# A four-layer graph kernel on one core: unread products in TensorE's first waits, layer 0's layernorms tied to mix copies, the first LSTM differences in a free tile, x loaded one group per iteration

## The chip, the cores and the metric

The kernel runs on one core of one Trainium2 chip. The core has five engines with instruction queues of their own: TensorE (PE in the profile, with its weight loads as PEld), VectorE (DVE), ScalarE (ACT), GpSimd (POOL) and SyncE (SP), which here only issues DMAs. The metric is the device time of one execution in microseconds, as a median over runs. All numbers are float32, and each float32 product is two instructions in the profile.

## The reference, cut to what matters

x is 128 graphs of 64 nodes with 256 features; adj is one 64 x 64 matrix for all graphs. Four layers follow each other, each as `x = x + layer(relu(layernorm(x)))`:

```
layer 0:  h = relu(adj @ (h @ Wg0 + bg0));  h = relu(adj @ (h @ Wg1 + bg1))
          for p in 1..4: an LSTM over windows of p nodes; its last state replaces each window's last node
layer 1:  4-head attention, masked by adj == 0
layer 2:  A_hat = normalized (adj + 1);  h = relu(batchnorm((A_hat @ h) @ W1.T + b1))
          out = batchnorm(h @ W2.T + b2)
layer 3:  w = adj * adj;  relu(w @ (h W1)), relu(w @ (h W2)), w @ (h W3)
```

## The kernel before, in words

The 8192 tokens lie as 16 groups (`NG`) of 512: a group is a tile of 128 partitions (two graphs of 64 nodes) x 4 token tiles (`GT`) x 256 features. Every stage loops over the 16 groups.

Products with a 64 x 64 matrix are made by `mix` (line 144, its two PSUM banks evicted at line 157): 32 small products, two batches side by side. Most large products use seven block products in place of eight (`seven`, lines 164 to 194): products 1, 5, 6 and 7 go to four PSUM banks, 1 and 5 are copied out at lines 173 and 174, and products 2, 3 and 4 follow in `finish`. Their operands need sums or differences of blocks, made on VectorE by `differences` (lines 198 to 202) or `sums` (206 to 209).

A layernorm is `ln_scale` followed by `ln_apply`: on VectorE four statistics (line 92), four aggregates (94), an addition (95); on GpSimd a power (96); on VectorE the shift (98); then four activations on ScalarE (111). A layernorm that is given `between` has its shift issued behind the instruction that `between` returns.

**Order.** The order on each engine is not that of the text. A list scheduler in the build gives each engine the first ready instruction by its own clock, and `tc.issue_after(ins)` puts what a block issues on ins's engine behind ins, as order alone and not as a wait. [...]SP's DMAs are in such a list as well.

**Layer 0's graph part** is a software pipeline (lines 465 to 471). In iteration g TensorE's text is: mix of group g (`first_mix`), second weights of group g-2 (line 453), second mix of group g-1 (line 144 again), first weights of group g (line 429). `first_mix` also holds the layernorm of its group. The first weights are followed by an addition on VectorE (437) and a relu on GpSimd (438), the second ones by an addition on VectorE (458) and a relu on ScalarE (461). All layernorms from group 2 on are put behind the first mix's copy alone. Before the loop, `by_batch` (297) turns adj, which comes in two DMAs, and `row_sums` (311 to 316) makes sums of it.

**The LSTMs** (line 507 on TensorE) read their differences from a tile of pool `dp`, which lies where the graph part's pools lay.

**The attention** has one iteration per group. ScalarE copies half the values out of PSUM (795, one buffer `vt`), and SP issues four 64 KB DMAs (798) that rearrange them into `v`; twice per iteration. Groups 4 to 15 of x are loaded again (512 KB each, line 58): four loads stand ahead of the loop and one in each of iterations 0 to 7. An iteration adds the LSTM result to x of group g+3 (`to_residual`) and makes the layernorm of group g+2; scores (814), exponentials (834), their transposes (850) and the weighted values (863) follow.

**Layer 2** starts in the attention's end: normalize (`activated`), mix, hidden products (735).

**Layer 3** starts while batchnorm's results (`outs`) are still being normalized (1083 on ScalarE, 1085 on VectorE), turned back (1095) and added to x (1103). `bring(n, ahead)` turns back and adds n groups and normalizes `ahead` more. `second_weights` (1222) is two sets of seven products; its differences t1 to t4 are made on VectorE. `finish` adds the last result (1301, 1308) and stores x (1304, 1309).

Of the kernel before, what the change touches and what calls it, by code (L numbers as in the profile page):

```python
# [8 lines left out]
F32 = mybir.dt.float32  # L9
# [5 lines left out]
P = 128  # L15
D = 256
NODES = 64
NTOK = 8192
GT = 4
# [5 lines left out]
NK = PER  # L25
# [13 lines left out]
def adj_preln_kernel(ctx: ExitStack, tc: tile.TileContext, x_in, adj, vec, bg0, bg1,  # L39
# [231 lines left out]
    with tc.tile_pool(name="lw", bufs=5) as lw:  # L271
# [6 lines left out]
        with tc.tile_pool(name="gw", bufs=1) as gw, tc.tile_pool(name="gcn", bufs=2) as gp, \  # L278
# [8 lines left out]
                )  # L287
            load_x(xs[1], 1)
            nc.sync.dma_start(out=vecs, in_=vec)
            ones = sp.tile([NODES, P], F32, tag="ones", name="ones")  # L290
            nc.vector.memset(ones, 1.0)

            def by_batch(ps, rows):

                for b in range(2):
                    blk = slice(b * 64, b * 64 + 64)
                    nc.tensor.matmul(
                        ps[blk, :], lhsT=rows[blk, :], rhs=ident[blk, blk], start=True, stop=True
                    )

            pt = bank((P, NODES))
            by_batch(pt, arow)
            lns = [
                ln_scale(xs[0][:, 0:2], lambda: nc.vector.tensor_copy(adj2, pt), 2),
                ln_scale(xs[0][:, 2:4], None, 2),
# [3 lines left out]
            def row_sums():  # L309
                pt1 = bank((P, NODES))  # L310
                nc.tensor.matmul(
                    pt1, lhsT=ones, rhs=adj2[0:NODES, :], start=True, stop=True
                )
# [54 lines left out]
                load_x(xs[g], g)  # L368
            w_next = (load_w(wih, 0), None)

            first_copied, first_scalar, middle_copied, turned = None, None, None, None

            def first_mix(g):
                nonlocal first_copied, middle_copied, first_scalar, turned
                h = gp.tile([P, GT, D], F32, tag="h", name="h")
                if g == 0:
                    for k, (rstd, nmr, _) in enumerate(lns):
                        two = slice(2 * k, 2 * k + 2)
                        ln_apply(xs[0][:, two], h[:, two], rstd, nmr, 2, (1,) if k else ())
                elif g == 1:  # L380
                    with tc.issue_after(first_copied):
                        rstd, nmr, _ = ln_scale(xs[1])
                    with tc.issue_after(first_scalar):
                        ln_apply(xs[1], h, rstd, nmr)
                    with tc.issue_after(first_copied):
                        row_sums()
                else:
                    if g < NK:
                        x = xs[g]
                    else:  # L390
                        x = gp.tile([P, GT, D], F32, tag="x", name="x", bufs=3)
                        load_x(x, g)
                    with tc.issue_after(first_copied):
                        ln_relu(x, h)
                m0 = gp.tile([P, 2, GN], F32, tag="m0", name="m0")
                if g == 0:


                    def on_scalar_first(*args):
                        nonlocal first_scalar  # L400
                        last = nc.scalar.copy(*args)
                        first_scalar = last.ins
                        return last

                    copied = mix(h, adj2, 2, m0, (on_scalar_first, on_vector))
                    first_copied = copied
                    with tc.issue_after(copied):
                        nc.vector.tensor_scalar(rb0[:, 0, :], rb0[:, 0, :], rsum, None, ALU.mult)
                else:
                    copied = mix(h, adj2, 2, m0, (on_vector, on_vector))  # L410
                if g == NG // 4:

                    with tc.issue_after(copied):
                        adjacency_forms()
                        turned = normalized_adjacency()
                if g == NG // 2:
                    middle_copied = copied
                    turned()
                return m0
# [23 lines left out]
                mix(h1, adj2, 2, m1, (on_scalar, on_vector if last else on_scalar))  # L443
                return m1

            def second_weights(g, m1):

                dst = hs[g // PER][:, :, :, (g % PER) * GB : (g % PER + 1) * GB]
                for m in range(2):
# [303 lines left out]
    with tc.tile_pool(name="att", bufs=2, reuse_waits="tile") as ap_:  # L753
# [136 lines left out]
        for g in range(NG):  # L890
# [105 lines left out]
    behind = [[], [], counted]  # L996
    for g in range(1, NG):
        if g == 1:
            mixed(2, (on_scalar, on_vector))
            behind.append(counted_next + hidden(1, w1, range(2, 4)))  # L1000
            continue
        if g + 1 < NG:
            with tc.issue_after(behind[g - 1][-1].ins if behind[g - 1] else after_attention):
                pool = ar_right if g + 1 < NG // 2 else keep if g + 1 == NG // 2 else ar_left
                activated(pool, g + 1, (lambda: behind[g][1]) if behind[g] else None)
                mixed(g + 1, (on_scalar, on_vector))
        if g == 3:
            for a in range(2):
# [286 lines left out]
    def finish(g, pss):  # L1295
        if g == NG - 1:

            for k in range(2):
                for q in range(2):
                    xt = xs[g][:, 2 * k + q, :]  # L1300
# [14 lines left out]
    def bring(n, ahead):  # L1315
# [14 lines left out]
    for g in range(NG + 1):  # L1330
# [78 lines left out]
```

## Time and profile before

| | |
|---|---|
| median of 3 runs (lowest, highest) | 2487.9 us (2487.6, 2489.17) |
| the profiled execution: device time | 2489.57 us |
| the profiled execution: span, first to last instruction | 2487.6 us |
| TensorE busy | 2450.4 us, 99% of the span |
| VectorE, ScalarE, GpSimd busy | 1512.0, 1149.8, 439.3 us |
| DMA | 48.00 MB, mean 19 GB/s |

A line of the timeline gives the start in us from the span's start, the busy time in us, engine, line, operation, tiles, shape and the number of instructions that were merged into it; in brackets stands the idle time of that engine before it and what ended the idle time. A line of the waits gives the waiting engine with its tile and line, what it waited for, then the sum in us, the number of times and the longest one.

### The profile page before, as it was taken

The page shows a single profiled execution, that of the slowest core. Times are in us where ns is not written, and L with a number is a line of the kernel's source. Part 1 is how long each engine was busy: PE and PEld are TensorE (multiplying, and loading weights), DVE is VectorE, ACT ScalarE, POOL GpSimd, SP SyncE. Part 2 cuts the span into 40 slices and gives each one's busy share as a digit, 9 for nine tenths or more (in the row PEclk, how much of TensorE's full clock was granted, in tenths as well). Part 3 has the DMA queues.
Part 4 walks back from the last instruction along what each step waited for, and adds up shares of the span by engine and source line. Part 5 has one row for each costly group of instructions (what it writes and reads, how often), then busy time and mean ns, then how long its engine had stood idle before and what let it go on. Part 6 is the DMA issues. An engine that isn't in the chain of part 4 may idle for free.

```text
span 2487.6 us, 46271 instructions
## 1 busy us (share of the span) xinstructions
PE 2450.4 (99%) x19626; PEld 2070.3 (83%) x19626; DVE 1512.0 (61%) x2703; ACT 1149.8 (46%) x2034; POOL 439.3 (18%) x368
## 2 busy tenths in 40 slices
PE   7999999999999999999999999999999999999999
PEld 5668888889999998888888864446998898888888
DVE  6658876666566565566589986425555455454544
ACT  4547754444455343344556566754333323333332
POOL 4422211111111111121134331003011111101110
PEclk9999999999999999999999999999999999999999
DMA  3200000001000000000311110010000000000000
GB/s 115 103 2 1 1 18 1 1 1 35 1 1 1 1 1 1 1 13 1 103 47 38 38 36 2 1 59 1 10 10 18 10 10 10 18 10 10 18 9 18
DMA packets 48527, 48.00 MB, mean 19 GB/s; under 512 B 3649, under 2 KB 44737, under 8 KB 48321
## 3 DMA queue, kind: packets, MB, share of 16 engines
q1 hardware_dynamic: 47616, 44.49, 5.8%
q8 instruction: 154, 2.52, 0.4%
q10 hardware_dynamic: 704, 0.56, 0.1%
q14 instruction: 53, 0.43, 0.1%
HBM read 28.26 MB, written 8.39 MB: 15 GB/s over the span
## 4 chain that ended last, share of the span: by engine, by line
PE 87%; DVE 7%; ACT 2%; POOL 2%; issue 1%; DMA 0%; SPq 0%; DVEq 0%; POOLq 0%; ACTq 0%
PE ps L507 40%; PE ps L1222 16%; PE ps L1267 8%; PE ps L1055 4%; PE ps L735 4%; PE ps L144 3%; PE ps L1186 3%; PE ps L429 2%; PE ps L453 2%; PE ps L768 2%; PE ps L790 1%; ACT arena L219 1%; DVE st L92 1%; POOL rstd L96 1%; POOL arena L180 1%
## 5 line engine op out<-in xcount | busy, mean ns | idle before, releaser
L507 PE MATMUL ps<-diff,s 128*128 128x256 f32 (+1 forms) x1824 | 393.5, 371 | 0.9 <-DVE diff L623 0.9
L1222 PE MATMUL ps<-arena 128*128 128x256 f32 x1792 | 392.6, 381 | 1.6 <-DVE arena L200 1.6
L1222 PEld LDWEIGHTS ps<-arena 128*128 128x128 f32 x1792 | 338.0, 190 | 55.7 <-issue 11.2
L507 PEld LDWEIGHTS ps<-diff,s 128*128 128x128 f32 x1824 | 346.0, 190 | 33.7 <-issue 1.6
L521 ACT ACTIVATE gates<-gates,lbias 128x512 f32<-128x512 f32 (+5 forms) x426 | 244.2, 621 | 202.5 <-DVE gates L185 146.9
L180 POOL TENSOR_TENSOR gates<-p 128x512 f32<-128x512 f32 (+1 forms) x115 | 149.2, 1297 | 882.1 <-DVE p L177 831.1
L507 PE MATMUL ps<-h,w 128*128 128x256 f32 (+1 forms) x1028 | 241.3, 371 | 1.6 <-ACT p L173 1.6
L507 PE MATMUL ps<-diff,w 128*128 128x256 f32 (+1 forms) x1040 | 238.7, 371 | 0.0
L507 PEld LDWEIGHTS ps<-diff,w 128*128 128x128 f32 x1040 | 197.4, 190 | 18.1
L507 PEld LDWEIGHTS ps<-h,w 128*128 128x128 f32 x1028 | 194.7, 190 | 20.8 <-ACT p L173 2.0
L521 ACT ACTIVATE gates<-ps,lbias 128x256 f32<-128x256 f32 (+3 forms) x213 | 91.7, 476 | 247.3 <-PE ps L507 247.2
L219 ACT ACTIVATE arena<-arena 128x512 f32<-128x512 f32 (+1 forms) x160 | 88.6, 582 | 195.2 <-POOL arena L180 103.2
L180 POOL TENSOR_TENSOR arena<-arena 128x512 f32<-128x512 f32 x64 | 73.1, 1143 | 530.6 <-DVE arena L177 530.6
L1267 PE MATMUL ps<-arena 128*128 128x128 f32 x1280 | 149.7, 276 | 0.0
L185 DVE TENSOR_TENSOR gates<-p,ps 128x512 f32<-128x512 f32 (+1 forms) x115 | 76.3, 664 | 120.2 <-PE ps L507 120.2
L1267 PEld LDWEIGHTS ps<-arena 128*128 128x128 f32 x1280 | 145.5, 192 | 1.1
L96 POOL TENSOR_TENSOR rstd<-rstd,mhalf 128x4 f32<-128x4 f32 (+1 forms) x66 | 66.4, 1006 | 412.1 <-DVE rstd L95 402.9
L185 DVE TENSOR_TENSOR arena<-arena,ps 128x512 f32<-128x512 f32 x64 | 39.7, 621 | 152.1 <-PE ps L1222 87.4
L176 DVE TENSOR_TENSOR p<-p,ps 128x512 f32<-128x512 f32 (+1 forms) x131 | 86.6, 661 | 51.2 <-PE ps L507 51.2
L507 PE MATMUL ps<-state,w 128*128 128x256 f32 (+1 forms) x512 | 116.1, 370 | 0.9 <-ACT p L173 0.8
L735 PE MATMUL ps<-arena,w 128*128 128x512 f32 x256 | 114.3, 599 | 1.9 <-ACT arena L157 1.9
L507 PE MATMUL ps<-state,s 128*128 128x256 f32 (+1 forms) x512 | 115.8, 369 | 0.0
(203 smaller groups left out, 4022.7 us busy)
## 6 DMA issues: line engine op xcount, KB each, us to landing
x<-in_x SPq DMA_DIRECT2D x27, 512.0 KB, 5.4
v<-vt SPq DMA_DIRECT2D x128, 64.0 KB, 2.1
out<-x SPq DMA_DIRECT2D x15, 512.0 KB, 2.9
w<-in_wih SPq DMA_DIRECT2D x4, 1024.0 KB, 7.4
w<-in_whh SPq DMA_DIRECT2D x3, 1024.0 KB, 6.0
arena<-in_l3w SPq DMA_DIRECT2D x3, 1024.0 KB, 5.1
w<-in_wqkv SPq DMA_DIRECT2D x1, 768.0 KB, 4.6
x<-in_x SPq DMA_DIRECT2D x2, 256.0 KB, 3.0
```

What stands on the lines that cost most here:

```text
L96: nc.gpsimd.tensor_tensor(out=rstd, in0=rstd, in1=mhalf[:, 0:n], op=ALU.pow)
L144: last = nc.tensor.matmul(pss[b][half * 64 : half * 64 + 64, c, t, :], lhsT=src[rows, t, col : col + 64], rhs=a2[rows, :], start=True, sto ...
L176: nc.vector.tensor_tensor(p1, p1, ps[2], ALU.add)
L180: nc.gpsimd.tensor_tensor(out=out[1][1], in0=p1, in1=p5, op=ALU.add)
L185: nc.vector.tensor_tensor(out[0][1], p1, ps[1], ALU.add)
L219: nc.scalar.activation(o, o, func)
L507: nc.tensor.matmul(ps[:, r], lhsT=wc[:, j, :], rhs=bc, start=first and r == 0 and c == 0, stop=True, skip_group_check=True,)
L521: nc.scalar.activation(o, ps, func, bias=lbias[:, col : col + 1])
L735: nc.tensor.matmul(ps, lhsT=w1[:, c, m * P : (m + 1) * P], rhs=a[:, 2 + c, :], start=(c == 0), stop=(c == 1),)
L1055: nc.tensor.matmul(pss[m], lhsT=w2[c // 2][:, c % 2, m * P : (m + 1) * P], rhs=a[:, c, :], start=(c == 0), stop=(c == 3),)
L1222: nc.tensor.matmul(ps[:, r, :], lhsT=w[:, c, col : col + P], rhs=b[:, c, :], start=first and r == 0 and c == 0, stop=c == 1, skip_group_ch ...
L1267: nc.tensor.matmul(ps[:, t, :], lhsT=w[:, c, t * P : (t + 1) * P], rhs=b[:, c, :], start=first and t == 0 and c == 0, stop=c == 3, skip_gr ...
```

## The change

It has eight edits, in the order of the program.

1. `ones` gets 128 partitions, and `keep_busy` issues products of `ones` with itself into a bank that nobody reads: seven ahead of `by_batch`, three behind its first product, two behind its second.
2. The layernorm of group g (from 2 on) is put on VectorE behind the second copy of mix g-2 (group 2's: behind group 1's shift), and its shift behind the second copy of mix g-1.
3. In iteration 16 the second weights of group 14 are cut in two, with the second mix of group 15 between the halves.
4. The differences of the first two LSTM units (p = 1) go into the tile "arena" of pool `keep`, which is free then.
5. Of x one group is loaded ahead of the attention, and group g+5 in iteration g.
6. Layer 2's mix of group 2 has both copies on ScalarE, and the later groups' work on ScalarE is put behind them.
7. In layer 3 `bring(2, 1)` after the first second mix becomes: turn the ready groups back into four banks there, and add them to x behind the differences of `second_weights`. Groups 5, 6 and 7 are normalized half on VectorE; before, both halves were ScalarE's.
8. The last group is stored in four DMAs of 128 KB, by turns from SP and from ScalarE, and no longer in two of 256 KB from SP.

```diff
-            ones = sp.tile([NODES, P], F32, tag="ones", name="ones")
+            ones = sp.tile([P, P], F32, tag="ones", name="ones")
...
-            def by_batch(ps, rows):
+            def by_batch(ps, rows, between=lambda b, last: None):
...
+                    between(b, last.ins)
+            idle = bank((P, P))
+            def keep_busy(n, behind=None):
+                with tc.issue_after(behind) if behind else nullcontext():
+                    for _ in range(n):
+                        nc.tensor.matmul(idle, lhsT=ones, rhs=ones, start=True, stop=True)
+            keep_busy(7)
             pt = bank((P, NODES))
-            by_batch(pt, arow)
+            by_batch(pt, arow, lambda b, last: keep_busy(3 - b, last))
...
-                        rstd, nmr, _ = ln_scale(xs[1])
+                        rstd, nmr, second_ln = ln_scale(xs[1])
...
-                    with tc.issue_after(first_copied):
-                        ln_relu(x, h)
+                    with tc.issue_after(second_ln if g == 2 else copied_of[g - 2].ins):
+                        ln_relu(x, h, lambda: copied_of[g - 1])
...
+                def on_vector_last(*args):
+                    copied_of.append(nc.vector.tensor_copy(*args))
+                    return copied_of[-1]
...
-                    copied = mix(h, adj2, 2, m0, (on_vector, on_vector))
+                    copied = mix(h, adj2, 2, m0, (on_vector, on_vector_last))
...
-            def second_weights(g, m1):
+            def second_weights(g, m1, ms=range(2)):
...
-                if m1 is not None:
-                    second_weights(g - 2, m1)
+                before = m1
+                if before is not None:
+                    second_weights(g - 2, before, range(1 if g == NG else 2))
                 m1 = second_mix(h1, g == NG) if h1 is not None else None
+                if g == NG:
+                    second_weights(g - 2, before, [1])
...
-                tt = dp.tile([P, 4, 2, 256], F32, tag="diff", name="diff")
+                pool, tag = (keep, "arena") if p == 1 and places[0] == units[0] else (dp, "diff")
+                tt = pool.tile([P, 4, 2, 256], F32, tag=tag, name="diff")
...
-        if g < 2 * NK:
+        if g == NK:
             load_x(xs[g], g)
...
-            if g + 2 * NK < NG:
-                load_x(xs[g + 2 * NK], g + 2 * NK)
+            if g + NK + 1 < NG:
+                load_x(xs[g + NK + 1], g + NK + 1)
...
-            mixed(2, (on_scalar, on_vector))
+            mixed_in = mixed(2, (on_scalar, on_scalar))
...
-                activated(pool, g + 1, (lambda: behind[g][1]) if behind[g] else None)
+                with tc.issue_after(mixed_in):
+                    activated(pool, g + 1, (lambda: behind[g][1]) if behind[g] else None)
...
-                two = slice(2 * k, 2 * k + 2)
-                t0 = g * GT + 2 * k
-                nc.sync.dma_start(out=out_view[:, t0 : t0 + 2, :], in_=xs[g][:, two, :])
+                    queue.dma_start(out=out_view[:, g * GT + t, :], in_=xt)
...
-                normalize(ready, on_scalar=range(2 if ready < NG // 2 else 1))
+                normalize(ready, on_scalar=range(2 if ready < 5 else 1))
...
             if g == 0:
-                bring(2, 1)
+                later = [(b, [bank((P, 2, D)) for _ in range(2)]) for b in range(brought, ready)]
+                for b, pss in later:
+                    turn_back(b, pss)
+                brought = ready
...
             h2, behind = second_weights(m1, h1)
+            if g == 0:
+                with tc.issue_after(behind):
+                    for b, pss in later:
+                        add_back(b, pss)
+                bring(0, 1)
             bring(1, 1)
```

More of the change, by code (lines that the diff above doesn't have):

```diff
@@ L289, in adj_preln_kernel @@
             nc.sync.dma_start(out=vecs, in_=vec)
-            ones = sp.tile([NODES, P], F32, tag="ones", name="ones")
+            ones = sp.tile([P, P], F32, tag="ones", name="ones")
             nc.vector.memset(ones, 1.0)
-            def by_batch(ps, rows):
+            def by_batch(ps, rows, between=lambda b, last: None):
                 for b in range(2):
                     blk = slice(b * 64, b * 64 + 64)
-                    nc.tensor.matmul(
+                    last = nc.tensor.matmul(
                         ps[blk, :], lhsT=rows[blk, :], rhs=ident[blk, blk], start=True, stop=True
                     )
+                    between(b, last.ins)
[5 more added lines that the diff above has]
+            keep_busy(7)
             pt = bank((P, NODES))
-            by_batch(pt, arow)
+            by_batch(pt, arow, lambda b, last: keep_busy(3 - b, last))
             lns = [
@@ L311, in row_sums @@
                 nc.tensor.matmul(
-                    pt1, lhsT=ones, rhs=adj2[0:NODES, :], start=True, stop=True
+                    pt1, lhsT=ones[0:NODES, :], rhs=adj2[0:NODES, :], start=True, stop=True
                 )
@@ L369, in adj_preln_kernel @@
             w_next = (load_w(wih, 0), None)
-            first_copied, first_scalar, middle_copied, turned = None, None, None, None
+            first_copied, first_scalar, middle_copied, turned, second_ln = [None] * 5
+            copied_of = []
             def first_mix(g):
-                nonlocal first_copied, middle_copied, first_scalar, turned
+                nonlocal first_copied, middle_copied, first_scalar, turned, second_ln
                 h = gp.tile([P, GT, D], F32, tag="h", name="h")
@@ L403, in on_scalar_first @@
                         return last
-                    copied = mix(h, adj2, 2, m0, (on_scalar_first, on_vector))
+                    copied = mix(h, adj2, 2, m0, (on_scalar_first, on_vector_last))
                     first_copied = copied
@@ L444, in second_mix @@
                 return m1
-            def second_weights(g, m1):
+            def second_weights(g, m1, ms=range(2)):
                 dst = hs[g // PER][:, :, :, (g % PER) * GB : (g % PER + 1) * GB]
-                for m in range(2):
+                for m in ms:
                     ps = bank((P, GB, NODES))
@@ L1298, in finish @@
             for k in range(2):
-                for q in range(2):
-                    xt = xs[g][:, 2 * k + q, :]
+                for q, queue in enumerate((nc.sync, nc.scalar)):
+                    t = 2 * k + q
+                    xt = xs[g][:, t, :]
                     nc.vector.tensor_tensor(xt, xt, pss[q][:, k, :], ALU.add)
-                two = slice(2 * k, 2 * k + 2)
-                t0 = g * GT + 2 * k
-                nc.sync.dma_start(out=out_view[:, t0 : t0 + 2, :], in_=xs[g][:, two, :])
+                    queue.dma_start(out=out_view[:, g * GT + t, :], in_=xt)
             return
```

## The prediction

> **What bounds the kernel now.** I read the page first, then TensorE's waits, then the timeline around each of them.
>
> ```profile
> span 2487.6 us, 46271 instructions
> PE 2450.4 (99%) x19626; PEld 2070.3 (83%) x19626; DVE 1512.0 (61%) x2703; ACT 1149.8 (46%) x2034; POOL 439.3 (18%) x368
> ...
> PE ps L297 <- DMA arow<-in_adj: 4.7, 2, 3.9
> PE ps L429 <- DVE m L157: 3.9, 2, 2.3
> ...
> PE ps L507 <- ACT p L173: 2.4, 3, 1.6
> PE ps L790 <- ACT hT L265: 2.3, 1, 2.3
> PE ps L735 <- ACT arena L157: 1.9, 1, 1.9
> PE ps L1222 <- DVE arena L200: 1.6, 1, 1.6
> PE ps L453 <- ACT m L157: 1.3, 1, 1.3
> ```
>
> TensorE is the bound everywhere: only 2487.6 - 2450.4 = 37.2 us of the span are without it. The change removes no product that is read, so it can win from those 37.2 us and from products that run slowly. The waits sit where stages begin, and every edit but one aims at one of them. The timeline shows the first:
>
> ```profile
> 9.66 5.94 PE L429 MATMUL ps<-wg,m 128*128 128x256 f32 x16 [0.89 <-ACT m L401]
> ...
> 12.65 0.43 DVE L92 BATCH_NORM_STATS2 st<-x 128x6 f32<-128x256 f32 x1 [1.00 <-DMA x<-in_x]
> ...
> 14.23 1.50 POOL L438 TENSOR_SCALAR h<-h 128x512 f32<-128x512 f32 x1 [7.78 <-DVE rstd L95]
> ...
> 15.69 1.04 POOL L96 TENSOR_TENSOR rstd<-rstd,mhalf 128x4 f32<-128x4 f32 x1
> ...
> 17.61 2.87 PE L144 MATMUL ps<-adj,h 64*64 64x64 f32 x128 [1.65 <-ACT h L111]
> ...
> 22.74 3.72 PE L429 MATMUL ps<-wg,m 128*128 128x256 f32 x16 [2.26 <-DVE m L157]
> ```
>
> The same sixteen instructions take 5.94 us at 9.66 and 3.72 us at 22.74. Group 1's layernorm is late: its aggregates end at 11.65, but its addition (L95) runs at 14.06, behind group 2's statistic, which waits for a DMA, and behind L437, which waits for the slow L429. Its power then queues behind a relu on GpSimd. Later layernorms that ran ahead also hold up the copies for L429 at 22.74 and at 33.91 (wait 1.63).
>
> [...]L429's instructions start 0.427 us apart until 14.06 and 0.216 after, and never slow down again. [...]here the two last 256 KB stores landed 2.2 and 2.3 us after issue.
>
> **The change, part by part.**
>
> 1. *Start (edits 1 and 2).* Seven unread products are fourteen instructions of 128 columns, half of L429's 256, so at the cold rate 14 x 0.213 = 3.0 us: from about 1.1 (`ones` is written at 0.81 to 0.98) to 4.1. `by_batch`'s first product waited for its DMA until 3.88, so it is 0.2 us later. Three more (1.3 us) push the second product, which started at 5.14, to 5.1 (warm) or 5.7 to 6.0 (cold). Behind it wait the copy of adj (L304), the shift (L98), the first activation and the first mix: that is the price of the fillers, 0 to 0.9 us. The last two end within the 1.5 us between `by_batch` and the mix. [...]The first mix then wins 0.45 us (its last eight-product group and tail), and L429 5.94 - 3.72 = 2.2. So L429 ends near 13.4, not 15.6.
> Group 2's statistics no longer stand ahead of L95. Group 1: statistics end at 11.4, aggregates 11.65, L95 11.8, power 12.9, shift 13.1, first activation 13.7. If L438 still gets GpSimd first, 1.5 to 2 us more; I take half: mix 1 starts at 14.5 and ends at 16.4. The second mix of group 0 needs the second relu (13.4 + 0.7 + 1.5 + 0.2 = 15.9) and ends at 17.4. Mix 1's copies (1.3) end at 17.8, so L429 of group 1 starts at about 17.9, 4.8 us before its 22.74. At 33.91 the copies are no longer behind layernorm work: 1.63 more, and 0.22 at 42.97. Sum **6.6**, bounds 4.4 (unread products leave the clock cold and cost 0.5) and 8.2 (power first, no push).
> Does the tie delay later groups? In the iteration at 47 to 57 the copies end at 50.6; shift 0.16 and four activations 2.08 end at 52.9 if ScalarE is free; the next mix is at 56.93. ScalarE's other work there (two L461, two copies, 3.3 us) fits ahead as well. Cost 0, with 0.8 us to spare in the worst order.
>
> 2. *Second weights cut (3).* The wait before L453 at 167.11 is 1.34 us: both copies of m after the last second mix. Half of L453 (1.85 us) now covers them. The mix may wait 0.15 us for L438 (ends 163.5). **1.1**; 0 if the half stays ahead of the mix, 1.3 at best.
>
> 3. *Differences (4).*
>
> ```profile
> 171.64 0.69 DVE L198 TENSOR_TENSOR diff<-h,h 128x512 f32<-128x512 f32 x1
> ...
> 173.26 0.70 PE L507 MATMUL ps<-h,w 128*128 128x256 f32 x2 [1.59 <-ACT p L173]
> ```
>
>    They need only groups 0 to 7, yet run behind the last L458. With nothing else to feed it, TensorE took part of product 2, which waits for L173. In a free tile the differences (four, 2.7 us) run in VectorE's idle time; products 5, 6 and 7 (12 x 0.216 = 2.6 us) cover L173. **1.5** of 1.59; 0 at worst.
>
> 4. *x loads (5).*
>
> ```profile
> 1219.34 2.75 SPq L58 DMA_DIRECT2D x<-in_x  x5
> 1225.02 2.64 SPq L798 DMA_DIRECT2D v<-vt  x4
> 1227.71 1.17 SPq L58 DMA_DIRECT2D x<-in_x  x2
> 1232.46 3.00 SPq L798 DMA_DIRECT2D v<-vt  x4
> 1235.50 2.29 SPq L58 DMA_DIRECT2D x<-in_x  x4
> 1237.98 2.82 SPq L798 DMA_DIRECT2D v<-vt  x4
> 1240.85 0.62 SPq L58 DMA_DIRECT2D x<-in_x  x1
> ...
> 1246.63 0.58 ACT L795 COPY vt<-ps 128x512 f32<-128x512 f32 x1 [2.54 <-DMA v<-vt]
> ```
>
>    Four v DMAs queued behind four x loads land 7.5 us after issue, not 2.1; L795 holds ScalarE, and TensorE waits 2.34 (L790) and, from the same delay, 1.04 (L850). But all twelve loads are issued by 1240.85, in iteration 1, though the last is written in iteration 7: SP takes a load as soon as its tile is free and no v DMA is ready. Writing the same twelve loads in later iterations changes neither. I take **0**; 3.4 if they do spread out. For a loss a load must come just ahead of the first v DMAs of an iteration, where L850 has no slack: (7.5 - 2.1)/4 = 1.35 us each, 14.9 for eleven. After a v batch SP idles over 3 us, so I give that little.
>
> 5. *Layer 2 (6).* L735 at 1476.97 waits for ScalarE's copy (1476.36), which stood behind three activations of group 3. Two copies at once after the mix (1475.1) take 0.1 + 0.57 + 0.5: L735 at 1476.35. **0.6** (0.3 to 0.9). The activations end 1 us later, at 1478.4; mix 3 is at 1484.04.
>
> 6. *Layer 3 (7).* VectorE ran L1103 four times (2.47 us) and L1085 between t1 and L199; TensorE waited 1.60 us for L200. Behind t4, the additions cover nothing of TensorE's. Four banks stay taken until about 1729; the second set of products needs banks at 1730.4. L1085 for groups 6 and 7 (2 x 0.54) falls into VectorE's 1.39 us idle before 1723.12. **1.6** (0.8 to 1.6).
>
> 7. *Store (8).* The last 128 KB in place of 256: **0.2** (-0.2 to 0.3)[...].
>
> **Sum**: 6.6 + 1.1 + 1.5 + 0 + 0.6 + 1.6 + 0.2 = 11.6 us. Against the profiled execution, 2489.57 (span 2487.6 and 1.97 around it), that is 2478.0; the median of the runs stands 1.67 lower: **2476.3 us**.
>
> **Rivals.**
> - *The x loads spread out.* For it: the stall is theirs. Against: SP's order above. 2476.3 - 3.4 = 2472.9.
> - *The start yields less*: GpSimd takes the relu first and the clock stays cold, or the halves of edit 3 stay together. 11.6 - 2.2 - 1.1 = 8.3: 2479.6; with both differences and halves lost, 2481.
> - *The tie becomes a wait per group.* Each shift now waits behind a copy. If that copy is queued 2.1 us late (two L437 and an L458 ahead of it), 0.8 us of slack is gone and groups 3 to 15 lose 1.3 us each: 17 us, against 11.6 won: 2493. It decides from 0.9 us per group on. Against it: VectorE is 60% busy there (70.67 of 117.20 us).
> - *The clock ignores the unread products*: within the second rival, 2478.5.
>
> **How the numbers follow.** My forecast 0.58; loads spread 0.22; less at the start or in the LSTM's entry 0.16; tie as a wait 0.04. A measurement of this kernel can tell about 0.2%, 5 us. Faster by more: all but the lowest part of the third case, 0.91. Within: 0.06. Slower: 0.03. The range runs from 2471 (loads spread, start at its upper bound) to 2481.5 (third case).
>
> **What would show it.** Right: L429's first sixteen near 3.7 us; group 1's L95 straight after its aggregates; no wait at L429 of group 2, at the last L453, at L1222; L507's first products followed by those with diff. Wrong: idle TensorE in every layer-0 group; L58 in other places among L798, with L790's wait gone.

## The result, and the profile after

| kernel | median (lowest to highest) | runs |
|---|---|---|
| before, beside the runs of the changed kernel | 2489.57 us (2487.6 to 2491.87) | 7 |
| changed | 2481.81 us (2479.47 to 2483.05) | 7 |
| ratio | 0.9967, 95% interval 0.9956 to 0.9979 | |

The change is faster by some 8 us of 2490, where 11.6 were forecast. The forecast started from the first three runs of the kernel before (2487.9) and so came out at 2476.3; the measured median lies 0.3 us above the upper end of the range, 2481.5. Taken from its own base the range was a gain of 6.4 to 16.9 us, and the measured 7.8 us lies in it, near its lower end.

The profiled execution took 2480.78 us. From the page of the changed kernel, span and busy time:

```profile
span 2479.0 us, 46321 instructions
...
PE 2454.4 (99%) x19650; PEld 2073.3 (84%) x19650; DVE 1513.1 (61%) x2705; ACT 1145.5 (46%) x2032; POOL 439.6 (18%) x368
```

TensorE is busy 4.0 us longer than before (2450.4): 3.35 + 1.53 + 0.71 us of unread products ("fillers" below) were added, the first sixteen L429 got 2.25 us shorter, and some products of layer 3 got longer (below). The span without TensorE fell from 37.2 to 24.6 us. Of TensorE's waits in the changed kernel (sum, times, longest) these are the first six lines without the third, which holds mixes of layers 2 and 3:

```profile
PE ps L1116 <- ACT arena L1104: 3.2, 2, 2.9
PE ps L810 <- ACT hT L265: 2.3, 1, 2.3
...
PE ps L144 <- POOL h L454: 1.8, 4, 0.8
PE ps L870 <- ACT e L854: 1.1, 1, 1.1
PE ps L308 <- DVE ones L291: 1.0, 1, 1.0
```

Lines moved with the edit: L429 is now L445, L437 and L438 are L453 and L454, L453 is L469, L507 is L526, the attention's L790, L795, L798, L814, L834, L850 are L810, L815, L818, L834, L854, L870, and layer 3's L1083, L1085, L1095, L1103, L1222 are L1104, L1106, L1116, L1124, L1243. The waits at the start (L297 4.7, now filled with unread products; L429 3.9), at the LSTM's entry (1.6), at the last L453 (1.3) and for L200 in layer 3 (1.6) are gone. The attention's two are where they were. On top stands a wait of 2.94 us that the kernel before didn't have.

The stages can be read apart. The landmarks are: the first L445 of group 1; a wait of 0.36 us for VectorE in the LSTMs, which both kernels have, near 535 us in the changed one and 542.5 us in the one before; the first product of the attention's queries and keys (L768 before, L788 changed); the first product with layer 2's second weights; the first L1116; the end of the last product.

| stage, from the profiled executions (us) | before | changed | won | forecast |
|---|---|---|---|---|
| A: start to group 1's first weights | 22.74 | 18.22 | 4.5 | 4.8 |
| B: rest of the graph part, LSTM's entry, to that wait | 519.79 | 516.42 | 3.4 | 4.45 |
| LSTMs | 678.35 | 678.34 | 0 | 0 |
| C: attention, first half of layer 2 | 367.81 | 364.20 | 3.6 | 0.6 |
| second half of layer 2 | 110.88 | 110.89 | 0 | 0 |
| D: layer 3 | 783.15 | 786.30 | -3.15 | 1.6 |
| after the last product | 4.85 | 4.62 | 0.2 | 0.2 |

The sum is 8.6 us, the difference of the spans. Start and B of the changed kernel's timeline:

```profile
1.04 3.35 PE L308 MATMUL ps<-ones 128*128 128x128 f32 x14 [1.04 <-DVE ones L291]
...
10.09 3.69 PE L445 MATMUL ps<-wg,m 128*128 128x256 f32 x16 [0.89 <-ACT m L417]
...
18.22 3.72 PE L445 MATMUL ps<-wg,m 128*128 128x256 f32 x16 [0.26 <-DVE m L409]
```

Both L445 now take 3.7 us and the second waits 0.26 us instead of 2.26. But 80 us later, in the timeline of group 9, there is something new:

```profile
96.55 0.66 DVE L198 TENSOR_TENSOR diff<-h,h 128x512 f32<-128x512 f32 x1
...
100.44 0.68 DVE L453 TENSOR_TENSOR h<-ps,rb 128x512 f32<-128x512 f32 x1
...
101.28 3.24 POOL L454 TENSOR_SCALAR h<-h 128x512 f32<-128x512 f32 x2 [2.81 <-DVE h L453]
...
103.12 0.69 PE L144 MATMUL ps<-adj,h 64*64 64x64 f32 x32 [0.43 <-POOL h L454]
...
104.57 0.69 PE L144 MATMUL ps<-adj,h 64*64 64x64 f32 x32 [0.76 <-POOL h L454]
```

The first LSTM's four differences run between 96.55 and 100.5, together with a sum of LSTM weights; another such sum stands between the two L453. L453, its relu L454 and the second mix come late: 1.2 us. Layer 3 of the same timeline shows the new wait:

```profile
1733.80 2.75 PE L1243 MATMUL ps<-arena 128*128 128x256 f32 x12
...
1738.11 0.63 ACT L219 ACTIVATE arena<-arena 128x512 f32<-128x512 f32 x1 [1.89 <-DVE arena L189]
1738.64 1.50 ACT L1104 ACTIVATE arena<-arena,n2sh,n2sc 128x512 f32<-128x512 f32 x2
...
1739.50 1.56 PE L1116 MATMUL ps<-ident,arena 128*128 128x128 f32 x8 [2.94 <-ACT arena L1104]
...
1740.98 1.99 PE L144 MATMUL ps<-w2s,arena 64*64 64x64 f32 x64
```

In the kernel before, the same place had no wait:

```profile
1749.40 1.04 PE L1095 MATMUL ps<-ident,arena 128*128 128x128 f32 x8
1750.37 1.16 PE L144 MATMUL ps<-w2s,arena 64*64 64x64 f32 x64
```

In the changed kernel TensorE has finished `second_weights` and comes to turning back group 8. Its normalize (L1104) stands on ScalarE behind the last relu of `second_weights` (L219, 1738.11). Then L1116 takes 1.56 us and the mix 1.99, against 1.04 and 1.16 before. The table of stretches tells why (time, TensorE's busy us; then the other engines; PEclk is the third value from the end):

```profile
1736.50:1740.00 3.50, 0.56 (x6) 0.50 (x6) 3.50 (x4) 1.89 (x3) 0.00 (x0) 1.00 0.00 0
1740.00:1743.40 3.40, 3.40 (x72) 2.95 (x71) 3.25 (x6) 0.49 (x2) 0.00 (x0) 0.50 0.00 0
```

The granted clock is one half for 3.41 us, from 1739.97 on. That stretch and the wait make up nearly all of the 4.75 us that layer 3 lacks against the forecast.

### The profile page after: what moved, and what is told of

It is laid out like the page before. It is cut to its first block, busy times and chain, and to the rows that moved or that the text cites. A ratio compares the mean times of both kernels' runs of the same rounds, so it can differ in the third digit from the quotient of the medians.

```text
span 2479.0 us, 46321 instructions
## 1 busy us (share of the span) xinstructions
PE 2454.4 (99%) x19650; PEld 2073.3 (84%) x19650; DVE 1513.1 (61%) x2705; ACT 1145.5 (46%) x2032; POOL 439.6 (18%) x368
## 4 chain that ended last, share of the span: by engine, by line
PE 84%; DVE 7%; ACT 2%; POOL 1%; issue 1%; DMA 0%; SPq 0%; DVEq 0%; POOLq 0%; ACTq 0%
PE ps L526 41%; PE ps L1243 16%; PE ps L1288 8%; PE ps L1076 4%; PE ps L755 4%; PE ps L144 3%; PE ps L1207 3%; PE ps L788 1%; PE ps L469 1%; PE ps L445 1%; ACT arena L219 1%; PE ps L810 1%; DVE st L92 1%; DVE e L853 1%; DVE mx L852 1%
## 5 line engine op out<-in xcount | busy, mean ns | idle before, releaser
L526 PE MATMUL ps<-diff,s 128*128 128x256 f32 (+1 forms) x1824 | 393.5, 371 | 0.9 <-DVE diff L643 0.9
L1243 PE MATMUL ps<-arena 128*128 128x256 f32 x1792 | 392.4, 380 | 0.0
L1243 PEld LDWEIGHTS ps<-arena 128*128 128x128 f32 x1792 | 337.9, 190 | 53.9 <-issue 9.2
L526 PEld LDWEIGHTS ps<-diff,s 128*128 128x128 f32 x1824 | 345.9, 190 | 33.8 <-issue 1.6
L526 PE MATMUL ps<-h,w 128*128 128x256 f32 (+1 forms) x1028 | 241.0, 371 | 0.0
L526 PE MATMUL ps<-diff,w 128*128 128x256 f32 (+1 forms) x1040 | 238.7, 370 | 0.0
L526 PEld LDWEIGHTS ps<-diff,w 128*128 128x128 f32 x1040 | 197.4, 190 | 18.2
L526 PEld LDWEIGHTS ps<-h,w 128*128 128x128 f32 x1028 | 194.7, 190 | 19.0 <-issue 0.5
L219 ACT ACTIVATE arena<-arena 128x512 f32<-128x512 f32 (+1 forms) x160 | 88.7, 582 | 193.1 <-POOL arena L180 101.2
L185 DVE TENSOR_TENSOR gates<-p,ps 128x512 f32<-128x512 f32 (+1 forms) x115 | 76.3, 664 | 120.0 <-PE ps L526 119.8
L526 PE MATMUL ps<-state,w 128*128 128x256 f32 (+1 forms) x512 | 116.1, 370 | 0.9 <-ACT p L173 0.8
L526 PE MATMUL ps<-state,s 128*128 128x256 f32 (+1 forms) x512 | 115.8, 369 | 0.0
L189 DVE TENSOR_TENSOR gates<-p,ps 128x512 f32<-128x512 f32 (+1 forms) x115 | 76.6, 666 | 63.9 <-PE ps L526 63.2
```

The source lines that it names most:

```text
L185: nc.vector.tensor_tensor(out[0][1], p1, ps[1], ALU.add)
L189: last = nc.vector.tensor_tensor(to, p, q, ALU.add)
L219: nc.scalar.activation(o, o, func)
L526: nc.tensor.matmul(ps[:, r], lhsT=wc[:, j, :], rhs=bc, start=first and r == 0 and c == 0, stop=True, skip_group_check=True,)
L1243: nc.tensor.matmul(ps[:, r, :], lhsT=w[:, c, col : col + P], rhs=b[:, c, :], start=first and r == 0 and c == 0, stop=c == 1, skip_group_ch ...
```

## The experiments

Each kernel ran five times or more, in three sets of four, beside the kernel before, whose median was 2490.78 (17 runs), 2491.37 and 2491.53 (9 each) in them. "Changed" is the changed kernel; it was measured beside 2489.57. Where two medians are compared below, the kernels' own are taken; by the ratios each experiment would stand 1.2 to 2.0 us better against changed. The intervals, some +-0.0013 or 3 us, leave single microseconds open. The stages carry the finer readings, but each comes from one profiled execution per kernel: B repeats to 0.3 us where nothing of it was altered, D to 0.1 us apart from the clock:

| kernel | median us | ratio (95%) | A | B | C | D |
|---|---|---|---|---|---|---|
| before | | 1 | 22.74 | 519.79 | 367.81 | 783.15 |
| changed | 2481.81 | 0.9967 (0.9956-0.9979) | 18.22 | 516.42 | 364.20 | 786.30 |
| normalize early | 2478.39 | 0.9947 (0.9933-0.9960) | 19.65 | 516.44 | 366.42 | 781.65 |
| edit 7 undone | 2479.99 | 0.9955 (0.9943-0.9968) | 18.01 | 516.37 | 365.56 | 783.16 |
| no unread products | 2482.34 | 0.9966 (0.9953-0.9978) | 19.33 | 516.50 | 363.92 | 786.39 |
| no tie | 2493.59 | 1.0011 (1.0002-1.0019) | 24.60 | 523.16 | 365.16 | 784.80 |
| edit 5 undone | 2481.45 | 0.9960 (0.9947-0.9972) | 18.34 | 516.45 | 365.05 | 784.88 |
| loads spread | 2481.74 | 0.9959 (0.9945-0.9972) | 19.32 | 516.59 | 363.78 | 786.38 |
| differences spread | 2481.03 | 0.9959 (0.9946-0.9971) | 18.74 | 515.04 | 365.24 | 786.35 |
| three repairs | 2474.45 | 0.9931 (0.9919-0.9944) | 18.59 | 514.82 | 363.58 | 781.70 |
| edit 4 undone | 2482.63 | 0.9963 (0.9950-0.9975) | 18.71 | 516.69 | 365.74 | 786.33 |
| edit 3 undone | 2483.06 | 0.9968 (0.9956-0.9981) | 18.21 | 517.43 | 366.72 | 784.83 |
| gap filled | 2482.03 | 0.9963 (0.9950-0.9975) | 19.16 | 516.31 | 365.73 | 785.01 |
| two repairs | 2477.05 | 0.9941 (0.9928-0.9955) | 19.61 | 514.82 | 365.44 | 781.71 |

**Normalize early.**

```
             if g == 0:
                 ...
                 brought = ready
+                bring(0, 1)
         ...
             h2, behind = second_weights(m1, h1)
             if g == 0:
                 with tc.issue_after(behind):
                     ...
-                bring(0, 1)
             bring(1, 1)
```

> The kernel after with one statement moved: group 8 of layer 3 is normalized ahead of the first group's second weights, as in the kernel before, not behind them. Theory A (ScalarE's queue): the 2.94 us wait of L1116 goes and, with no pause of that length left, TensorE keeps its full clock, which gave away another 1.6 us: 4.5 us less than after, near 2477.5 us. Theory B (the pause does not cause the half clock): the wait goes and the half clock stays: 2.9 us less. Theory C (the wait is for VectorE's additions or for a bank of PSUM that they free): the wait only changes its name: within 1 us of after. A counter-effect to look for: the two activations (1.5 us) may now stand ahead of the copy that L1243's differences need; then L1243 waits up to 1.6 us.

Layer 3 fell from 786.30 to 781.65: 4.65 us, as theory A has it. TensorE's timeline of this kernel at the same place:

```profile
1737.71 2.54 PE L1243 MATMUL ps<-arena 128*128 128x256 f32 x11
1740.08 1.04 PE L1116 MATMUL ps<-ident,arena 128*128 128x128 f32 x8
1741.05 1.16 PE L144 MATMUL ps<-w2s,arena 64*64 64x64 f32 x64
```

No wait, no slow product, and L1243's first wait doesn't come back either: the counter-effect is absent. The median is 3.4 us lower than that of changed (5 by the ratios), and this profile shows a new place for the half clock. Its stretches (same columns):

```profile
1239.00:1243.00 4.00, 0.94 (x4) 0.72 (x5) 0.89 (x3) 1.56 (x3) 0.00 (x0) 0.98 0.47 100
1243.00:1246.30 3.30, 3.30 (x10) 2.54 (x9) 3.20 (x6) 0.26 (x1) 0.00 (x0) 0.50 0.29 72
```

The wait at L810 was 3.07 us in this execution, and 3.41 us of half clock followed. Of the ten experiments that have the same loads there as changed or before, six show a half-clock stretch behind that wait in their profile and four, like changed itself, don't.

**Edit 7 undone.** `bring(2, 1)` is back behind `second_mix`, the turn-backs and additions behind `second_weights` are gone, and ScalarE gets both chunks up to group 7 again.

> The kernel after with edit 7 (layer 3) undone and all else kept. By the comparison of the two traces, edit 7 took 1.6 us away at L1243 and cost 2.94 us of waiting and about 1.6 us of half clock: without it the kernel is 3 us faster than after, near 2479, with L200's wait of 1.6 us back and the granted clock at full speed throughout layer 3. By the step of the prediction it would be 1.6 us slower, near 2483.5.

From TensorE's waits of this kernel:

```profile
PE ps L1243 <- DVE arena L200: 1.6, 1, 1.6
```

Layer 3 takes 783.16 us, that of the kernel before to 0.01 us, and L1243's wait of 1.60 us is back. So edit 7 cost 3.15 us in the profiled execution, 1.5 of it only where the clock is lost. The prediction's step has the wrong sign as a whole. Its mechanism isn't wrong: with the normalize put early, edit 7 wins 783.15 - 781.65 = 1.5 us.

**No unread products.** `keep_busy(7)` and the two calls between `by_batch`'s products are out.

> The kernel after without the twelve unread products at the start, the tie kept. If they warm the clock: the first sixteen L445 take about 5.9 us again and the first mix starts some 0.9 us earlier, the clock is full only from about 14 us on, and the sum is 1.3 to 2 us slower than after. If the unread products don't count for the clock, or if the early work alone would have warmed it: 0.9 us faster than after (their price goes, nothing is lost).

The median can't tell it from changed. In the profile the first sixteen L444 (L445 before the edit) take 6.07 us, and the clock is full from 14.77 us on; group 1's begin at 19.33. With the products that landmark is 18.01 to 18.74 in seven executions that got the full clock at 4.3 to 6.6 us, 19.16 and 19.32 in two at 10.0 and 10.5, 19.65 and 19.61 in two at 14.1 and 14.0. The mean of the eleven is 18.78: against the single execution without fillers they are worth about 0.55 us, 1.3 at best, and cost 0.3 where they fail. Why the executions differ so isn't settled: in those that got the full clock at 14 us TensorE had worked without a pause from 1.04 to 9.9.

**No tie.** The tie is edit 2, the order that it sets for the layernorms.

```
-                    with tc.issue_after(second_ln if g == 2 else copied_of[g - 2].ins):
-                        ln_relu(x, h, lambda: copied_of[g - 1])
+                    with tc.issue_after(first_copied):
+                        ln_relu(x, h)
```

> The kernel after with groups 2 and up tied as before (all behind the first copy only), the unread products kept. If the tie is what wins at groups 1 to 3: the waits ahead of L445 in groups 1 and 2 come back (2.3 and 1.6 us, and 0.2 in group 3), 4 to 5 us slower than after; L95 of group 1 stands behind the statistics of group 2 again. If the warm clock alone brought most of the gain: within 2 us of after. If the tie also delays later groups by a little each: less than 4 us, with idle TensorE in after's groups that this kernel lacks.

11 (by the ratios) to 12 us slower than changed, and slower than the kernel before: more than any of the theories said. TensorE's waits of this kernel, three of the first five lines:

```profile
PE ps L144 <- POOL h L454: 3.3, 3, 2.7
...
PE ps L144 <- ACT h L111: 2.4, 2, 2.1
...
PE ps L445 <- DVE m L409: 2.3, 1, 2.3
```

The waits of the start are back, 2.06 and 2.25 us. A third, 2.68 us at 112.2, is not known from the kernel before: between the two additions of group 9 VectorE runs one of the differences of edit 4 and a shift (112.49) that waits 2.38 us for its power; the power (1.03 us) itself stands on GpSimd behind the first relu. The clock is lost behind the waits too. Two of its stretches:

```profile
26.00:29.00 3.00, 3.00 (x9) 2.37 (x8) 2.40 (x11) 2.08 (x4) 1.34 (x3) 0.51 0.01 3
...
114.30:121.00 6.70, 6.11 (x44) 5.01 (x45) 3.96 (x14) 3.05 (x4) 1.59 (x3) 0.50 0.01 2
```

The clock is halved from 8.4 to 15.3 us, from 25.5 to 28.9 and from 114.3 to 121.1: 17 us at half speed. The stages show it: A is 5.8 us above the mean of the tied kernels (18.78) and B 6.7 above changed. Part of A is chance: the second half of adj came late in this execution, so that `by_batch`'s second product started at 7.18 us and not at 6.19. With the other edits in place the tie is worth its waits and the clock behind them. Nothing here supports a tie that turned into a wait per group.

**Edit 5 undone.** The loads stand in the text as before.

> The kernel after with edit 5 (x loads) undone, all else kept. If, as the prediction said, SP takes a load as soon as its tile is free wherever it is written: the order on SP stays x4 to x8, four v DMAs, x9 and so on, L810 waits 1.4 to 3 us as in after, and the time is within 1 us of after (near 2481.8). If writing the loads one per iteration did spare something (after had 0.64 us of TensorE's issue pauses in attention, before had 3.3): 1.5 to 2.7 us slower.

No difference. SP's queue in the changed kernel, for comparison with the lines shown of before:

```profile
1211.45 2.62 SPq L58 DMA_DIRECT2D x<-in_x  x5
1217.13 2.64 SPq L818 DMA_DIRECT2D v<-vt  x4
...
1227.38 2.29 SPq L58 DMA_DIRECT2D x<-in_x  x4
1230.09 2.69 SPq L818 DMA_DIRECT2D v<-vt  x4
1232.82 0.59 SPq L58 DMA_DIRECT2D x<-in_x  x1
```

The same five, two, four and one, and again four v DMAs behind four loads: issued from 1230.1 on, landed at 1237.7 to 1238.6. With edit 5 undone the queue shows the same counts. L810 waits 2.12 us. So what C won in the changed kernel's profile beyond edit 6 is not shown to be edit 5's. C lies between 363.9 and 366.7 in the eleven executions (changed and ten experiments) that differ in nothing there but edit 5. TensorE's waits explain this scatter: take away their sum, and 1.5 us where a half-clock stretch followed L810, and 358.7 to 359.5 us are left in all of them, and 359.3 in the kernel before. The largest difference to before is at L834, where TensorE paused without a releaser that the profile shows: 3.3 us in the one execution of before, 0.6 to 1.9 in the others.

**Loads spread.**

```
-            values(hT_all, v, (1,))
+            sent = values(hT_all, v, (1,))
+            if g + NK + 1 < NG:
+                with tc.issue_after(sent):
+                    load_x(xs[g + NK + 1], g + NK + 1)
```

(`values` returns its last v DMA, and the load behind the first `values` is out)

> The kernel after with each x load of attention tied behind the last v DMA of its own iteration, so that the loads really are issued one per iteration. If the x loads delay the v DMAs: L795's counterpart gets its v DMAs about 2.2 us after issue, the waits at L810 (1.4 to 3.1 us in the runs so far) and L870 (1.0) go, and with the first any half-clock stretch behind it: 3.3 us less than after, near 2478.5; up to 5 in executions where that wait had cost the clock. If they only happen to stand beside the waits, which come from the entry of the stage itself: within 1 us of after. If eleven loads in the way of later v DMAs cost more than one jam at the start: slower than after by up to 10 us.

Now SP's queue has one load for each eight v DMAs:

```profile
1218.42 8.01 SPq L818 DMA_DIRECT2D v<-vt  x8
1226.47 0.59 SPq L58 DMA_DIRECT2D x<-in_x  x1
1228.71 11.24 SPq L818 DMA_DIRECT2D v<-vt  x8
1240.00 1.26 SPq L58 DMA_DIRECT2D x<-in_x  x1
```

The wait of L810 is gone. But in this kernel's timeline (lines from L811 on are one or two higher than in changed) one takes its place:

```profile
1228.09 0.59 ACT L815 COPY vt<-ps 128x512 f32<-128x512 f32 x1 [3.83 <-DMA v<-vt]
...
1229.67 1.28 ACT L855 ACT_TABLE_LOAD   x1
...
1232.08 1.09 PE L871 MATMUL ps<-ident,e 128*128 128x128 f32 x8 [1.17 <-ACT e L855]
```

ScalarE still waits for v DMAs at the entry, since the copy's only buffer has to be emptied (3.83 us), and the exponential stands behind it with its table load (1.28 us). C is 363.78, and 363.58 in the kernel with three repairs, against a mean of 365.38 over the other eleven: 1.7 us, half of the 3.4 that the rival promised; both lie below the lowest of the eleven, 363.92. The median shows nothing of it.

**Differences spread.** Each of the four first differences is put behind the second copy of another mix, of groups 10 to 13.

> The kernel after with the four first LSTM differences each tied behind the copy of another group (10 to 13), not all in one stretch of VectorE's queue ahead of group 9's additions L453. If that stretch (six instructions of 0.68 us, four of them the differences) made L454 late: the waits of 0.43 and 0.76 us at 102.7 and 103.8 go, no others come, and the LSTM begins 1.2 us earlier: 1.2 us less than after, near 2480.6. If the power and the relu on GpSimd set these waits whatever stands on VectorE: the same two waits stay and the time is that of after within 0.5.

```profile
99.75 3.70 PE L476 MATMUL ps<-m,wg 128*128 128x512 f32 x8 [0.36 <-ACT m L157]
103.39 1.16 PE L144 MATMUL ps<-adj,h 64*64 64x64 f32 x64
```

B fell by 1.38 us to 515.04; the waits of 0.43 and 0.76 us are gone. A wait of 0.36 us came before the second weights (L476 here, L469 in the changed kernel); the two later kernels with the same repair don't have it, and their B is 514.82. The median is 0.8 lower, which its interval can't tell from nothing.

**Three repairs.** Normalize early, loads spread, differences spread.

> The kernel after with three repairs at once: group 8 normalized ahead of the second weights (as in the experiment before), x loads spread over the iterations, first differences spread over four groups. If the three costs are separate, their gains add: 3 to 4.5 (normalize) + 3.3 (loads) + 1.2 (differences) = 7.5 to 9 us less than after, near 2473.5, with no half-clock stretch after the start in most executions. If a later wait takes the place of the loads' wait, 3 less of that: near 2476.5.

2474.45 us (2473.38 to 2474.67), ratio 0.9931 to the kernel before, interval 0.9919 to 0.9944: 17 us faster than before and, with intervals that don't overlap, faster than the changed kernel: by 7.4 us by the medians, 9 by the ratios. The mean granted clock was 1.000 in all five runs. B and D have their repaired values at once.

**Edit 4 undone.**

> The kernel after with edit 4 undone: the first LSTM differences are again in the rotating tile, behind the last additions. If edit 4 won 1.6 us at the LSTM's first product and lost 1.2 us at the waits for L454 at 102.7 and 103.8: both change back, net 0.4 us slower than after, near 2482.2, with a wait of about 1.6 us at the first L526 and none at 102 to 104. By the prediction's step alone: 1.5 us slower.

B is 516.69, 0.27 longer than in changed: L526 waits 1.60 us, and nothing at 102 to 104. The first theory holds.

**Edit 3 undone.**

> The kernel after with edit 3 undone: the last but one group's second weights are again in one piece ahead of the last second mix. By the prediction's step: the wait of 1.3 us before the last L469 comes back, 1.1 us slower than after. If the half that was moved only shifted the wait to the mix ahead of it: no difference.

B is 517.43, 1.01 longer, with a wait of 1.34 us at the last L469. The prediction's step holds. In this execution the wait of 2.94 us at L1116 (here L1114) is there, but no half clock follows, and D is 784.83 instead of 786.30:

```profile
1743.03 1.09 PE L1114 MATMUL ps<-ident,arena 128*128 128x128 f32 x8 [2.94 <-ACT arena L1102]
1744.05 1.16 PE L144 MATMUL ps<-w2s,arena 64*64 64x64 f32 x64
```

So the half clock behind L1116 cost 1.5 us by itself.

**Gap filled.**

```
             ps = {k: bank((P, 2, D))}
+            if g == 8 and k == 0:
+                with tc.issue_after(sent[0].ins):
+                    for _ in range(6):
+                        nc.tensor.matmul(ps[k][:, 0, :], lhsT=ident, rhs=b1[0][0], start=True, stop=True)
             turn_back(g, ps, ks=[k])
```

(`sent[0]` is the last product of `second_weights`; the first case is that the pause itself brings the half clock)

> The kernel after with six unread products (twelve instructions of 256 columns, 12 x 0.216 = 2.6 us) placed on TensorE behind the first group's last L1243, in the pause before L1116 of group 8; what that L1116 waits for is unchanged. [...]L1116 starts at the same distance behind L1243 as in after, the half-clock stretch of 3.41 us does not come, and the time is 1.6 us less than after, near 2480.2. If the stretch comes for another reason (for instance the load of the other engines): the same time as after. If the products delay L1116: up to 1 us slower.

TensorE's timeline of this kernel (L1132 are the unread products):

```profile
1738.78 2.75 PE L1132 MATMUL ps<-arena,ident 128*128 128x256 f32 x12
...
1741.88 1.09 PE L1116 MATMUL ps<-ident,arena 128*128 128x128 f32 x8 [0.35 <-ACT arena L1104]
1742.90 1.16 PE L144 MATMUL ps<-w2s,arena 64*64 64x64 f32 x64
```

L1116 starts 2.94 us behind L1243's end, as in changed, and it and the mix run at full speed; D is 785.01, 1.3 us less, the value of the executions in which the clock wasn't lost. But this doesn't show that the products kept the clock: with edit 3 undone the same wait of 2.94 us, with nothing in it, was followed by the full clock too. So the experiment leaves open what covering the gap is worth. The median doesn't show 1.3 us either; in this profile half clock came behind L810's wait of 2.78 us.

**Two repairs.** The three without the spread loads.

> The kernel with the three repairs without the one of the x loads: group 8 normalized early and the first differences spread, x loads as in after. If the loads' repair is worth only what the waits in attention show (0.2 us by the traces of the kernel with that repair alone): within 1 us of the kernel with three, near 2475. If its worth is that the wait of 1.8 to 3.1 us at the first L810 costs a half-clock stretch in about half of the executions: 1 to 2.5 us slower than with three, and more scatter (2474 to 2478). If 3.3 us: near 2477.8 in every execution.

2477.05 us (2476.52 to 2477.26): 2.6 more than with three repairs, and the runs of the two kernels don't overlap. In the two profiled executions, 2.9 us apart, 1.9 us is C (365.44 against 363.58: L810 waits 1.97 us and the half clock follows); 1.0 is A, where this execution got the full clock at 14.0 us and the other at 6.6. The second theory fits the size; its larger scatter isn't there.

## Why the prediction was right and wrong, step by step

- **Start (edits 1 and 2):** right in size, wrong in its shares. Group 1's first weights were forecast at 17.9 and began at 18.22 (18.0 to 19.7 over the executions with the tie). The forecast gave the fillers about 2 us net and the tie the rest. Measured, the fillers give 0.55 on average: the forecast counted on the full clock for group 0's first weights (3.72 us, not 5.94), and in four of eleven executions it came at 10 to 14 us. How soon it would come with them, the trace of the kernel before doesn't show. The tie carries most of the gain: with it and without fillers A is 19.33, 3.4 us below the kernel before. Fillers without the tie gave 24.60, the lost clock and the late adj included. In stage B it brought 519.79 - 516.42 - 1.01 - 0.27 = 2.1 us, forecast 1.63 + 0.22.
- **Second weights cut (3):** 1.0 measured, 1.1 forecast. Right.
- **First differences (4):** the step that failed is "the differences run in VectorE's idle time". L526's wait did go (1.6 us), but the scheduler put all four in one stretch ahead of L453, and TensorE lost 1.2 us there; 0.27 was left of 1.5. Spread over four groups they give 1.65. VectorE was idle enough on average (the prediction counted it 60% busy), but not between the statistics and the addition that the second mix needs.
- **x loads (5):** right, by the order on SP that the kernel before already showed. The rival's price, 3.4 us if they do spread, was twice too large: it summed the two waits and did not ask what ScalarE would do next. Behind the jam stand the copy's single buffer (a wait of 3.83 us) and the table load (1.28 us), and 1.7 us is what remains.
- **Layer 2 (6):** L735's wait of 1.86 us became a wait of 0.88 at the next mix, and of 0.67 to 0.69 in most other executions. About 1.1 us, forecast 0.6. C's other gain in the profile, some 2.5 us, was not forecast. It sits in L834's pauses (3.3 us before, 0.6 changed); no run ties them to an edit, there is one execution of the kernel before, and the stage scatters by 2.8 us from one execution to the next.
- **Layer 3 (7):** the step that failed most: 1.6 us were forecast to be won, 3.15 were lost in the profiled execution. The 1.6 us at L200 was sized rightly (1.5 with the repair). What was left out is the last line of the edit: `bring(0, 1)`, the normalize of group 8, moves behind `second_weights`, whose ScalarE work then stands ahead of it, while its turn-back on TensorE stays where it was. The prediction listed the additions and L1085 on VectorE and the banks, but not ScalarE's queue, in which the normalize that a later product waits for now stands behind `second_weights`. Price: 2.94 us plus 1.5 of clock and 0.2 not traced further, together 4.65.
- **Store (8):** 0.2, as forecast: the last four DMAs of 128 KB landed 1.75 to 1.87 us after issue, where the two of 256 KB took 2.19 and 2.27. That size would change little the trace of the kernel before shows too: its v DMAs of 64 KB took 2.1 us in the median.
- **The clock.** The prediction priced every wait at its length, since in the kernel before the clock stayed full from 14 us to the last product, behind waits of 2.26 us (L429 at 22.74) and 2.34 us (L790) too. That was not so in other kernels: 3.41 us of half clock followed the wait of 2.94 us at L1116 in changed and that of 3.07 us at L810 with the normalize early, and without the tie the waits of 2.25 and 2.68 us at 24.60 and 114.89 had 3.4 us of it from 25.5 on and 6.8 us from 114.3 on. The forecast has nothing for it; at L1116 it was 1.5 us.

The rivals: the tie as a wait per group did not appear; loads that spread by being written later neither; "less at the start or at the LSTM's entry" is what happened at the LSTM's entry, for another reason than the two given. The direction was never in doubt, since the waits at the start are large and the layernorm's order explains them. That the total comes as near to the forecast as it does is partly luck: in the profiled execution layer 3 came out 4.75 us worse than forecast and C 3.0 us better, and neither was foreseen.

## What to carry to other kernels

When a step is moved past another one, list for each engine what stands ahead of it in its new place, and start with the instruction that the bounding engine needs first. A wait on TensorE can have a second price, the half clock behind it: at L1116 a wait of 2.94 us cost 1.5 us more in five of eight executions. Such a wait is worth removing first. Whether covering it with unread products pays was not shown here. A stage that scatters by 3 us from one execution to the next must be compared over several traces before a gain in it is believed.

## What the runs showed of the hardware that was not expected

The same wait of TensorE was followed by half clock in one execution and by full clock in another. Eight of the profiled executions have the wait of 2.94 us at L1116 with nothing put into it, and TensorE and the other engines do the same work there each time. In five of them (changed, no unread products, loads spread, differences spread, edit 4 undone) half clock followed, and D took 786.30 to 786.39 us; in three (no tie, edit 5 undone, edit 3 undone) the clock stayed full, and D took 784.80 to 784.88 us.

It was so at L810 too. With the normalize early, its wait of 3.07 us was followed by half clock, and in the gap-filled kernel one of 2.78 us; in changed 2.27 us was followed by full clock, and so were the 2.34 us at the same place (L790) in the kernel before. The length of a wait alone doesn't tell what follows it: the eight at L1116 are equally long. What does was not shown.
